# Reordering the first batch's opening, delaying one step of the second batch, and splitting the last output of a fused linear-attention and dense-experts kernel

## The chip, the core and the metric

The kernel runs on one core of one Trainium2 chip. The core has a matmul engine (TensorE, PE in the profile; its weight loads are listed as PEld), a vector engine (VectorE, DVE), an activation engine (ScalarE, ACT), a general engine (GpSimd, POOL), and SyncE (SP), which here only issues transfers. Each runs its own list of instructions in order and waits on semaphores for the others. Matmul results land in PSUM[...]. The metric is the device time of the whole program in microseconds (us); lower is better.

## What is computed

Eight batches of 512 tokens with 128 channels go through a linear attention block and then through eight dense experts, each with a layer norm before and after and a residual. All data are float32. This is the core of the reference:

```python
def attn(x, gamma, beta, w_qkv, w_out, b_out):        # x: (8, 512, 128)
    xn = (x - mean(x)) / sqrt(var(x) + 1e-5) * gamma + beta
    q, k, v = split(xn @ w_qkv, 3)                     # each as 4 heads of 32
    q = q * 32 ** -0.5
    k = softmax(k, axis=tokens)
    context = einsum('bnhd,bnhe->bhde', k, v)
    out = einsum('bhde,bnhd->bnhe', context, q)        # back to 128 channels
    return out @ w_out + b_out + x

def ffn(x, Wg, Wu, Wd):                                # 8 experts, hidden 512
    return sum(silu(x @ Wg[e]) * (x @ Wu[e]) @ Wd[e] for e in range(8))

x = x + layernorm(attn(layernorm(x), ...))
x = x + layernorm(ffn(layernorm(x), Wg, Wu, Wd))
```

## The kernel before

The work is staged by batch. The experts' part is a loop over *units*: a unit is one batch, but the first and the last batch are cut into two halves of 256 tokens each, so there are ten units. Every unit has 32 steps (8 experts by 4 slices of the hidden 512). A step multiplies the slice's `wg` and `wu` with the unit's normalised tokens `zT` (L572, L574), takes the silu of the first product on ACT (L576), multiplies the two on DVE (L578), and, two steps later, multiplies the result with `wd` into an accumulator bank (L532, function `down`). The tile framework is in manual schedule: every engine executes its instructions in exactly the order in which the program text issues them, and the framework only adds the waits.

Everything else is written as Python generators that are advanced once per step by `between`: `attention(b + 1)` for the next batch, `finish` for the output of the unit before, and for the first unit `prepare` (products of weights) and the rest of the first batch's second half. So a `yield` in one of these generators means "let one step of the experts go by".

`opening()` is the first batch's attention, which has no other work to hide behind. It works in two halves (`h` = 0, 1) of 256 tokens: statistics and normalisation on DVE (`xh`), transposes on PE (`xh_ps`), scale and shift on ACT (`xnT`); then for each half the product for `k` and the product for `v`; the maximum of `k` over the tokens (`kmax`, DVE) with copies of `v` on ACT; the products for `q`; the exponential of `k` (`ekT`, ACT); transposes of it (`ek_ps`) and copies (`ek`); the scaling of `q` (`qT`, ACT); and a one-element silu (`junk`) that makes ACT load the silu table. Then the chain `c_ps` (k times v), `ctxT` (mask to heads), `m_ps` (times w_out), `m` (divided by the softmax sum). `x1b` is the normalised input plus the output bias, added per 128 tokens on POOL (L303).

`after_wa` is the tail of attention for a range of tokens, again a generator: `y` = `q` times `m` on PE into the bank `y_ps` (L472) plus `x1b` on DVE (L476); statistics of `y`; `yn` and `x2`, the first residual; statistics of `x2`; `z`; transposes `z_ps`; and one ACT copy into `zT` (L495). `opening` advances the first half (`first`) to its end and the second half (`second`) up to its statistics; the rest of it runs during the first unit's steps. Five calls of `keep_warm` issue matmuls whose result is never read, two at the start and three in the tail.

In the attention of batch 1 (`b in BY_TENSORE`), the transposes of the exponential are copied from `ek_ps` to `ek` on DVE (L417), and one `yield` later the matmuls `g_ps` (L429) use it. In batches 2 to 7 the exponential goes through DRAM instead, and several steps are let by.

At the end of the program, the last unit's accumulator is copied whole to `fT` (L540, DVE), and `finish` transposes its two blocks of 128 tokens into one bank `f_ps`, takes statistics, normalises (`fn`), adds `x2` on POOL (L517) and issues one output transfer on SP's queue (L518).

Of the kernel before, what the change touches and what calls it, by code (L numbers as in the profile page):

```python
# [8 lines left out]
F32 = mybir.dt.float32  # L9
AF = mybir.ActivationFunctionType  # L10
# [5 lines left out]
def kernel(  # L16
# [223 lines left out]
    def flat(t):  # L240
        return t.rearrange("p j c -> p (j c)")
# [6 lines left out]
    def opening():  # L248


        b, xt = 0, xs[0]
        banks = [(ps, "ps"), (ps_gu, "g"), (ps_gu, "u")]
        turn = [0]

        def bank(name):
            pool, tag = banks[turn[0] % 3]
            turn[0] += 1
            return pool.tile([P, N], F32, tag=tag, name=f"{name}_{b}")
# [10 lines left out]
        x2s[0] = x2  # L269
        y = work.tile([P, NJ, C], F32, tag="y", name="y_0")  # L270
        yn = work.tile([P, NJ, C], F32, tag="yn", name="yn_0")
# [3 lines left out]
        ksum = small.tile([P, 3], F32, tag="ksum0", name="ksum_0")  # L275
        rsum = small.tile([P, 1], F32, tag="rsum", name="rsum_0")
        H = range(2)
        J = [slice(lo, hi) for lo, hi in HALVES]
        COL = [slice(lo * P, hi * P) for lo, hi in HALVES]
        W = N // 2  # L280

        keep_warm(warm, 2)
        keep_warm(w_qkv_sb[:, : N // 2])
# [5 lines left out]
        for h in H:  # L289
            norm_apply(xh[:, J[h]], xt[:, J[h]], (s1[h][0], s1[h][2]))  # L290
            t = bank(f"xh_ps{h}")
            for j in H:
                nc.tensor.transpose(t[:, j * P : (j + 1) * P], xh[:, 2 * h + j, :], ident)
            nc.scalar.activation(
                xnT[:, COL[h]], t[:, :W], AF.Identity, bias=beta_sb, scale=gamma_sb
            )
# [11 lines left out]
        for h in H:  # L308
            k_ps.append(bank(f"k_ps{h}"))
            nc.tensor.matmul(  # L310
                k_ps[h][:, :W], w_qkv_sb[:, C : 2 * C], xnT[:, COL[h]], start=True, stop=True
            )
            v_ps.append(bank(f"v_ps{h}"))
            for j in H:
                nc.tensor.matmul(
                    v_ps[h][:, j * C : (j + 1) * C],
                    xnT[:, (2 * h + j) * P : (2 * h + j + 1) * P], w_qkv_sb[:, 2 * C : 3 * C],
                    start=True, stop=True,
                )
        for h in H:  # L320
            nc.vector.tensor_reduce(kmax[:, h : h + 1], k_ps[h][:, :W], AX.X, ALU.max, negate=True)
            nc.scalar.copy(v[:, COL[h]], v_ps[h][:, :W])
        nc.vector.tensor_tensor(kmax[:, 2:3], kmax[:, 0:1], kmax[:, 1:2], ALU.min)
        for h in H:
            q_ps.append(bank(f"q_ps{h}"))
            nc.tensor.matmul(
                q_ps[h][:, :W], w_qkv_sb[:, 0:C], xnT[:, COL[h]], start=True, stop=True
            )
        for h in H:
            nc.scalar.activation(  # L330
                ekT[:, COL[h]], k_ps[h][:, :W], AF.Exp, bias=kmax[:, 2:3],
                accum_out=ksum[:, h : h + 1],
            )
        first_norm(1)
        for h in H:
            t = bank(f"ek_ps{h}")
            for j in H:
                nc.tensor.transpose(
                    t[:, j * P : (j + 1) * P], ekT[:, (2 * h + j) * P : (2 * h + j + 1) * P], ident
                )  # L340
            (nc.scalar.copy if h else nc.vector.tensor_copy)(ek[:, COL[h]], t[:, :W])
        for h in H:
            nc.scalar.mul(qT[:, COL[h]], q_ps[h][:, :W], QSCALE)
        nc.scalar.activation(junk, warm[:, :1], AF.Silu)
        nc.vector.tensor_tensor(ksum[:, 2:3], ksum[:, 0:1], ksum[:, 1:2], ALU.add)
        nc.vector.reciprocal(rsum, ksum[:, 2:3])
        c_ps = bank("c_ps")
        for j in range(NJ):
            nc.tensor.matmul(
                c_ps[:, :C], v[:, j * C : (j + 1) * C], ek[:, j * C : (j + 1) * C],  # L350
                start=(j == 0), stop=(j == NJ - 1),
            )
        ctxT = work.tile([P, C], F32, tag="ctxT", name="ctxT_0")
        nc.vector.tensor_tensor(ctxT, c_ps[:, :C], heads, ALU.mult)
        m_ps = bank("m_ps")
        nc.tensor.matmul(m_ps[:, :C], ctxT, w_out_sb, start=True, stop=True)
        m = work.tile([P, C], F32, tag="m", name="m_0")
# [18 lines left out]
    def attention(b):  # L376
# [38 lines left out]
        if b in BY_TENSORE:  # L415
            ek_ps = transpose4(ekT, f"ek_ps_{b}")
            nc.vector.tensor_copy(  # L417
                ek.rearrange("p b (j k) -> p j b k", j=NJ),
                ek_ps.rearrange("p (j b k) -> p j b k", j=NJ, b=NQ),
            )  # L420
# [47 lines left out]
    def after_wa(b, lo, hi, xt, xnT, wa, x1b, x2, y, yn, z, zT):  # L468
        r = slice(lo, hi)
        y_ps = ps.tile([P, N], F32, tag="ps", name=f"y_ps_{b}_{lo}")  # L470
        for j in range(lo, hi):
            nc.tensor.matmul(  # L472
                y_ps[:, (j - lo) * C : (j - lo + 1) * C], xnT[:, j * P : (j + 1) * P], wa,
                start=True, stop=True,
            )
        nc.vector.tensor_tensor(  # L476
            flat(y[:, r]), y_ps[:, : (hi - lo) * C], flat(x1b[:, r]), ALU.add
        )
# [13 lines left out]
        if b in BY_TENSORE:  # L492
            yield
            z_ps = transpose4(flat(z[:, r]), f"z_ps_{b}_{lo}")
            nc.scalar.copy(zT[:, :, r], by_block(z_ps[:, : (hi - lo) * P], hi - lo))  # L495
            zTs[b, lo] = zT[:, :, r]
# [5 lines left out]
    def finish(b, lo, hi, f):  # L502
# [15 lines left out]
        nc.sync.dma_start(out[b].rearrange("(p j) c -> p j c", j=NJ)[:, r], o[:, :n])  # L518

    units = [(b, lo, hi) for b in range(B) for lo, hi in parts(b)]  # L520
    NSTEP = E * NF
# [4 lines left out]
    def down(n, i):  # L526
# [19 lines left out]
    def between(n):  # L546
# [10 lines left out]
        for i in range(NSTEP):  # L557
            if i == LAG + 1 and n > 0:
                going.append(finish(*units[n - 1], fTs.pop(n - 1)))
            going = [g for g in going if next(g, "end") != "end"]  # L560
            yield

    opening()
# [57 lines left out]
```

## Time and profile before

| | us |
|---|---|
| median of 3 runs | 721.32 (721.27 to 721.45) |
| the profiled execution, its own time | 721.76 |
| its span, first to last instruction | 719.8 |
| PE busy in the span | 705.7 (98%) |
| DVE, ACT, POOL busy | 311.7, 200.9, 75.5 |

The profile is of one execution. Its span is divided by what it does: the opening ends with the first matmul of the experts (L572) at 22.70 us; from there the ten units follow one another until the last `down` matmul, at about 712.9; the end is what comes behind it. A row of the timeline gives the start in us, the duration, the engine, the line and the operation, and in brackets how long the engine had been idle before it and who released it. Float32 matmuls appear as two instructions each, so `x2` is one matmul. A busy engine is one with an instruction in flight; [...]the distance between the starts of two matmuls is shorter than the duration of one.

### The profile page before, as it was taken

What the parts mean: (1) busy time and instruction counts of PE and PEld (TensorE: products, weight loads), DVE (VectorE), ACT (ScalarE), POOL (GpSimd) and SP (SyncE); (2) the same over time, 40 slices, a digit from 0 to 9 for tenths busy, and PEclk for the clock granted to TensorE, in tenths of its full rate; (3) what the DMA queues carried; (4) which work ended last, traced back from release to release, by engine and by line L of the source; (5) the groups of instructions that cost most, each with busy time, mean ns of one, the idle gap of its engine ahead of it and who ended that gap; (6) DMA issues with size and microseconds to landing.
All of it is one profiled execution on the core that took longest, in us unless ns stands there. A gap on an engine that the chain in (4) does not pass through costs nothing. (4 is left out here: it accounts for less than half of the span.)

```text
span 719.8 us, 6734 instructions
## 1 busy us (share of the span) xinstructions
PE 705.7 (98%) x2177; PEld 397.7 (55%) x2177; DVE 311.7 (43%) x872; ACT 200.9 (28%) x378; POOL 75.5 (10%) x101
## 2 busy tenths in 40 slices
PE   7899999999999999999999999999999999999996
PEld 5788786444444544445444444444444454488885
DVE  4534545435345352444444444443534535243433
ACT  3323332422224122241223322242222412222221
POOL 3100111101002010020100110010100201000000
PEclk9999999999999999999999999999999999999999
DMA  8400000010110001110101101010001100000000
GB/s 268 145 1 0 23 1 15 22 31 0 44 60 34 11 15 29 59 45 0 45 8 51 45 0 44 30 45 30 0 29 47 42 15 12 18 31 15 8 1 8
DMA packets 27299, 23.83 MB, mean 33 GB/s; under 512 B 2944, under 2 KB 20480, under 8 KB 27264
## 3 DMA queue, kind: packets, MB, share of 16 engines
q1 hardware_dynamic: 27120, 23.28, 10.0%
q8 instruction: 17, 0.28, 0.2%
q14 instruction: 18, 0.15, 0.1%
q10 hardware_dynamic: 144, 0.13, 0.1%
HBM read 15.01 MB, written 8.39 MB: 33 GB/s over the span
## 5 line engine op out<-in xcount | busy, mean ns | idle before, releaser
L578 DVE TENSOR_TENSOR h<-sg,u 128x512 f32<-128x512 f32 (+1 forms) x320 | 185.4, 581 | 357.4 <-PE u L574 339.3
L576 ACT ACTIVATE sg<-g 128x512 f32<-128x512 f32 (+1 forms) x320 | 163.5, 511 | 481.8 <-PE g L572 445.1
L572 PE MATMUL g<-zT,wg 128*128 128x512 f32 (+1 forms) x640 | 272.6, 507 | 0.7 <-ACT zT L495 0.5
L574 PE MATMUL u<-zT,wu 128*128 128x512 f32 (+1 forms) x640 | 272.3, 507 | 0.0
L532 PE MATMUL acc<-h,wd 128*128 128x512 f32 (+1 forms) x640 | 272.1, 507 | 0.1
L532 PEld LDWEIGHTS acc<-h,wd 128*128 128x128 f32 x640 | 121.4, 190 | 99.3 <-issue 91.8
L574 PEld LDWEIGHTS u<-zT,wu 128*128 128x128 f32 x640 | 121.3, 190 | 98.9 <-issue 86.3
L572 PEld LDWEIGHTS g<-zT,wg 128*128 128x128 f32 x640 | 118.3, 190 | 84.5 <-issue 77.0
L172 POOL TENSOR_TENSOR rstd<-ve,mhalf 128x4 f32<-128x4 f32 (+1 forms) x28 | 25.9, 926 | 394.3 <-DVE ve L170 394.2
L194 POOL TENSOR_TENSOR rstd<-ve,mhalf 128x8 f32<-128x8 f32 x7 | 11.5, 1637 | 185.6 <-DVE ve L187 185.6
L412 POOL TENSOR_TENSOR x1b<-x,bias_sb 128x128 f32<-128x128 f32 x28 | 12.1, 462 | 23.1 <-DVE x L200 23.1
L517 POOL TENSOR_TENSOR o<-fn,x 128x512 f32<-128x512 f32 (+1 forms) x10 | 10.5, 1050 | 20.7 <-DVE fn L200 18.9
L200 DVE TENSOR_SCALAR x<-x,mv,rstd 128x128 f32<-128x128 f32 x32 | 11.1, 406 | 0.1
L483 POOL TENSOR_TENSOR x<-yn,x 128x512 f32<-128x512 f32 (+1 forms) x8 | 9.6, 1201 | 11.8 <-DVE yn L200 10.5
L200 DVE TENSOR_SCALAR xh<-x,mv,rstd 128x128 f32<-128x128 f32 x32 | 8.8, 336 | 2.1 <-POOL rstd L194 1.8
L429 PEld LDWEIGHTS g_ps<-ek,xh 128*128 128x128 f32 x56 | 7.3, 191 | 4.5 <-issue 2.9
L168 DVE BATCH_NORM_AGGREGATE mv<-stats 128x2 f32<-128x6 f32 x96 | 9.6, 157 | 0.0
L200 DVE TENSOR_SCALAR z<-x,mv,rstd 128x128 f32<-128x128 f32 x32 | 9.0, 341 | 1.3 <-POOL rstd L172 1.3
L200 DVE TENSOR_SCALAR yn<-y,mv,rstd 128x128 f32<-128x128 f32 x32 | 9.0, 341 | 1.3 <-POOL rstd L172 1.3
L476 DVE TENSOR_TENSOR y<-y_ps,x1b 128x512 f32<-128x512 f32 (+1 forms) x9 | 5.7, 632 | 8.2 <-PE y_ps L472 8.2
L404 ACT ACT_TABLE_LOAD x7 | 9.0, 1283 | 0.1
L576 ACT ACT_TABLE_LOAD x7 | 9.0, 1283 | 0.1
(115 smaller groups left out, 199.9 us busy)
## 6 DMA issues: line engine op xcount, KB each, us to landing
wg<-in_L_ffn_Wg_dram SPq DMA_DIRECT2D x8, 256.0 KB, 6.0
wu<-in_L_ffn_Wu_dram SPq DMA_DIRECT2D x8, 256.0 KB, 5.9
wd<-in_L_ffn_Wd_dram SPq DMA_DIRECT2D x8, 256.0 KB, 6.1
x<-in_L_attn_x_dram SPq DMA_DIRECT2D x7, 256.0 KB, 2.8
bounce<-xh_blk SPq DMA_DIRECT2D x6, 256.0 KB, 2.0
xhT<-bounce SPq DMA_DIRECT2D x24, 64.0 KB, 2.0
bounce<-ek_blk SPq DMA_DIRECT2D x6, 256.0 KB, 2.0
ek<-bounce SPq DMA_DIRECT2D x24, 64.0 KB, 2.0
```

Source lines behind the costliest of these rows:

```text
L168: nc.vector.bn_aggr(mv[:, j, :], stats[:, j, :])
L172: nc.gpsimd.tensor_tensor(rstd, ve, mhalf[:, :n], ALU.pow)
L194: nc.gpsimd.tensor_tensor(rstd, ve, mhalf, ALU.pow)
L200: nc.vector.tensor_scalar(dst[:, j], src[:, j], mv[:, j, 0:1], rstd[:, j : j + 1], ALU.subtract, ALU.mult,)
L412: nc.gpsimd.tensor_tensor(x1b[:, j, :], x1[:, j, :], bias_sb, ALU.add)
L483: (nc.gpsimd if b or lo else nc.vector).tensor_tensor(flat(x2[:, r]), flat(yn[:, r]), flat(xt[:, r]), ALU.add)
L517: nc.gpsimd.tensor_tensor(flat(o[:, :n]), flat(fn[:, :n]), flat(x2s[b][:, r]), ALU.add)
L532: nc.tensor.matmul(accs[n][:, :cols], wd_sb[e][:, f, :], hs.pop((n, i)), start=(i == 0), stop=(i == NSTEP - 1),)
L572: nc.tensor.matmul(g_ps[:, :cols], wg_sb[e][:, w], zT, start=True, stop=True)
L574: nc.tensor.matmul(u_ps[:, :cols], wu_sb[e][:, w], zT, start=True, stop=True)
L576: nc.scalar.activation(sg[:, :cols], g_ps[:, :cols], AF.Silu)
L578: nc.vector.tensor_tensor(h[:, :cols], sg[:, :cols], u_ps[:, :cols], ALU.mult)
```

## The change

The opening no longer takes its PSUM banks in turn from a list of three; every call of `bank` names its pool. The dummy matmuls at the start are four instead of two. Both products for `k` and their maxima are issued ahead of the products for `v`; the exponentials are issued ahead of the copies of `v`, and these copies move from ACT to DVE. The products for `q` and their scaling move behind `c_ps` and behind `m_ps`, one half each. For batch 0, `after_wa` adds `x1b` on PE: a matmul of the identity with `x1b` into `y_ps` comes first (for the first half ahead of the transposes of the exponential), the product `q` times `m` is accumulated on top, and statistics and normalisation read `y_ps` itself; the DVE addition is gone. One dummy matmul pair reads `xt` where it read `y`. The copy of the first half's transposed `z` is cut in two, one block on ACT, one on DVE. In the attention of batch 1 a second `yield` stands between `ek` and `g_ps`. The last unit gets a function of its own, `finish_last`, which copies, transposes, normalises, adds and stores its two blocks of 128 tokens one by one, the first block stored from SP's queue and the second from ACT's.

```diff
@@ -249,12 +249,9 @@
         b, xt = 0, xs[0]
-        banks = [(ps, "ps"), (ps_gu, "g"), (ps_gu, "u")]
-        turn = [0]
-
-        def bank(name):
-            pool, tag = banks[turn[0] % 3]
-            turn[0] += 1
+        def bank(name, tag):
+            pool = ps if tag == "ps" else ps_gu
             return pool.tile([P, N], F32, tag=tag, name=f"{name}_{b}")
 
...
-        y = work.tile([P, NJ, C], F32, tag="y", name="y_0")
+        y = {}
         yn = work.tile([P, NJ, C], F32, tag="yn", name="yn_0")
         z = work.tile([P, NJ, C], F32, tag="z", name="z_0")
         zT = work.tile([P, NQ, NJ, Q], F32, tag="zT", name="zT_0")
         kmax = small.tile([P, 3], F32, tag="kmax0", name="kmax_0")
         ksum = small.tile([P, 3], F32, tag="ksum0", name="ksum_0")
         rsum = small.tile([P, 1], F32, tag="rsum", name="rsum_0")
+        m = work.tile([P, C], F32, tag="m", name="m_0")
+        first, second = [
+            after_wa(b, lo, hi, xt, qT, m, x1b, x2, y, yn, z, zT) for lo, hi in HALVES
+        ]
         H = range(2)
         J = [slice(lo, hi) for lo, hi in HALVES]
         COL = [slice(lo * P, hi * P) for lo, hi in HALVES]
         W = N // 2
 
-        keep_warm(warm, 2)
+        keep_warm(warm, 4)
         keep_warm(w_qkv_sb[:, : N // 2])
         nc.scalar.copy(junk, warm[:, :1])
         s1 = [pair_stats(xt[:, J[h]], f"1_0_{h}") for h in H]
@@ -288,7 +289,7 @@
         q_ps = []
         for h in H:
             norm_apply(xh[:, J[h]], xt[:, J[h]], (s1[h][0], s1[h][2]))
-            t = bank(f"xh_ps{h}")
+            t = bank(f"xh_ps{h}", "g" if h else "ps")
             for j in H:
                 nc.tensor.transpose(t[:, j * P : (j + 1) * P], xh[:, 2 * h + j, :], ident)
             nc.scalar.activation(
@@ -306,63 +307,60 @@
 
         first_norm(0)
         for h in H:
-            k_ps.append(bank(f"k_ps{h}"))
+            k_ps.append(bank(f"k_ps{h}", "ps" if h else "u"))
             nc.tensor.matmul(
                 k_ps[h][:, :W], w_qkv_sb[:, C : 2 * C], xnT[:, COL[h]], start=True, stop=True
             )
-            v_ps.append(bank(f"v_ps{h}"))
+            nc.vector.tensor_reduce(kmax[:, h : h + 1], k_ps[h][:, :W], AX.X, ALU.max, negate=True)
+        nc.vector.tensor_tensor(kmax[:, 2:3], kmax[:, 0:1], kmax[:, 1:2], ALU.min)
+        for h in H:
+            nc.scalar.activation(
+                ekT[:, COL[h]], k_ps[h][:, :W], AF.Exp, bias=kmax[:, 2:3],
+                accum_out=ksum[:, h : h + 1],
+            )
+        for h in H:
+            v_ps.append(bank(f"v_ps{h}", "u" if h else "g"))
             for j in H:
                 nc.tensor.matmul(
                     v_ps[h][:, j * C : (j + 1) * C],
                     xnT[:, (2 * h + j) * P : (2 * h + j + 1) * P], w_qkv_sb[:, 2 * C : 3 * C],
                     start=True, stop=True,
                 )
+            nc.vector.tensor_copy(v[:, COL[h]], v_ps[h][:, :W])
+        next(first)
         for h in H:
-            nc.vector.tensor_reduce(kmax[:, h : h + 1], k_ps[h][:, :W], AX.X, ALU.max, negate=True)
-            nc.scalar.copy(v[:, COL[h]], v_ps[h][:, :W])
-        nc.vector.tensor_tensor(kmax[:, 2:3], kmax[:, 0:1], kmax[:, 1:2], ALU.min)
-        for h in H:
-            q_ps.append(bank(f"q_ps{h}"))
-            nc.tensor.matmul(
-                q_ps[h][:, :W], w_qkv_sb[:, 0:C], xnT[:, COL[h]], start=True, stop=True
-            )
-        for h in H:
-            nc.scalar.activation(
-                ekT[:, COL[h]], k_ps[h][:, :W], AF.Exp, bias=kmax[:, 2:3],
-                accum_out=ksum[:, h : h + 1],
-            )
-        first_norm(1)
-        for h in H:
-            t = bank(f"ek_ps{h}")
+            t = bank(f"ek_ps{h}", "u" if h else "g")
             for j in H:
                 nc.tensor.transpose(
                     t[:, j * P : (j + 1) * P], ekT[:, (2 * h + j) * P : (2 * h + j + 1) * P], ident
                 )
             (nc.scalar.copy if h else nc.vector.tensor_copy)(ek[:, COL[h]], t[:, :W])
-        for h in H:
-            nc.scalar.mul(qT[:, COL[h]], q_ps[h][:, :W], QSCALE)
-        nc.scalar.activation(junk, warm[:, :1], AF.Silu)
-        nc.vector.tensor_tensor(ksum[:, 2:3], ksum[:, 0:1], ksum[:, 1:2], ALU.add)
-        nc.vector.reciprocal(rsum, ksum[:, 2:3])
-        c_ps = bank("c_ps")
+        first_norm(1)
+        c_ps = bank("c_ps", "g")
         for j in range(NJ):
             nc.tensor.matmul(
                 c_ps[:, :C], v[:, j * C : (j + 1) * C], ek[:, j * C : (j + 1) * C],
                 start=(j == 0), stop=(j == NJ - 1),
             )
+        q_ps.append(bank("q_ps0", "u"))
+        nc.tensor.matmul(q_ps[0][:, :W], w_qkv_sb[:, 0:C], xnT[:, COL[0]], start=True, stop=True)
+        nc.scalar.mul(qT[:, COL[0]], q_ps[0][:, :W], QSCALE)
         ctxT = work.tile([P, C], F32, tag="ctxT", name="ctxT_0")
         nc.vector.tensor_tensor(ctxT, c_ps[:, :C], heads, ALU.mult)
-        m_ps = bank("m_ps")
+        m_ps = bank("m_ps", "ps")
         nc.tensor.matmul(m_ps[:, :C], ctxT, w_out_sb, start=True, stop=True)
-        m = work.tile([P, C], F32, tag="m", name="m_0")
+        q_ps.append(bank("q_ps1", "g"))
+        nc.tensor.matmul(q_ps[1][:, :W], w_qkv_sb[:, 0:C], xnT[:, COL[1]], start=True, stop=True)
+        nc.scalar.mul(qT[:, COL[1]], q_ps[1][:, :W], QSCALE)
+        nc.scalar.activation(junk, warm[:, :1], AF.Silu)
+        nc.vector.tensor_tensor(ksum[:, 2:3], ksum[:, 0:1], ksum[:, 1:2], ALU.add)
+        nc.vector.reciprocal(rsum, ksum[:, 2:3])
         nc.vector.tensor_scalar(m, m_ps[:, :C], rsum, None, ALU.mult)
-        first, second = [
-            after_wa(b, lo, hi, xt, qT, m, x1b, x2, y, yn, z, zT) for lo, hi in HALVES
-        ]
-        next(first)
         next(first)
         next(second)
-        keep_warm(flat(y[:, J[0]]), 2)
+        next(second)
+        keep_warm(flat(xt[:, J[0]]), 2)
+        next(first)
         next(first)
         keep_warm(flat(yn[:, J[0]]), 2)
         next(first)
@@ -418,6 +416,7 @@
                 ek.rearrange("p b (j k) -> p j b k", j=NJ),
                 ek_ps.rearrange("p (j b k) -> p j b k", j=NJ, b=NQ),
             )
+            yield
             yield
         else:
             to_tokens(by_block(ekT), ek, f"ek_blk_{b}")
@@ -468,18 +467,26 @@
     def after_wa(b, lo, hi, xt, xnT, wa, x1b, x2, y, yn, z, zT):
         r = slice(lo, hi)
         y_ps = ps.tile([P, N], F32, tag="ps", name=f"y_ps_{b}_{lo}")
+        if b == 0:
+            for j in range(lo, hi):
+                cols = slice((j - lo) * C, (j - lo + 1) * C)
+                nc.tensor.matmul(y_ps[:, cols], ident, x1b[:, j, :], start=(j == lo), stop=False)
+            yield
         for j in range(lo, hi):
             nc.tensor.matmul(
                 y_ps[:, (j - lo) * C : (j - lo + 1) * C], xnT[:, j * P : (j + 1) * P], wa,
-                start=True, stop=True,
-            )
-        nc.vector.tensor_tensor(
-            flat(y[:, r]), y_ps[:, : (hi - lo) * C], flat(x1b[:, r]), ALU.add
-        )
-        yield
-        s3 = norm_stats(y[:, r], f"3_{b}_{lo}")
-        yield
-        norm_apply(yn[:, r], y[:, r], s3)
+                start=(b > 0), stop=(b > 0 or j == hi - 1),
+            )
+        if b == 0:
+            y[lo] = y_ps[:, : (hi - lo) * C].rearrange("p (j c) -> p j c", c=C)
+            yb = y[lo]
+        else:
+            yb = y[:, r]
+            nc.vector.tensor_tensor(flat(yb), y_ps[:, : (hi - lo) * C], flat(x1b[:, r]), ALU.add)
+        yield
+        s3 = norm_stats(yb, f"3_{b}_{lo}")
+        yield
+        norm_apply(yn[:, r], yb, s3)
         (nc.gpsimd if b or lo else nc.vector).tensor_tensor(
             flat(x2[:, r]), flat(yn[:, r]), flat(xt[:, r]), ALU.add
         )
@@ -492,7 +499,12 @@
         if b in BY_TENSORE:
             yield
             z_ps = transpose4(flat(z[:, r]), f"z_ps_{b}_{lo}")
-            nc.scalar.copy(zT[:, :, r], by_block(z_ps[:, : (hi - lo) * P], hi - lo))
+            for j in range(hi - lo if b == 0 and lo == 0 else 1):
+                cp = nc.vector.tensor_copy if j else nc.scalar.copy
+                if b or lo:
+                    cp(zT[:, :, r], by_block(z_ps[:, : (hi - lo) * P], hi - lo))
+                else:
+                    cp(zT[:, :, j], z_ps[:, j * P : (j + 1) * P].rearrange("c (a i) -> c a i", a=NQ))
             zTs[b, lo] = zT[:, :, r]
         else:
             to_channels(z, zT.rearrange("c a j i -> c a (j i)"), f"z_blk_{b}")
@@ -517,6 +529,44 @@
         nc.gpsimd.tensor_tensor(flat(o[:, :n]), flat(fn[:, :n]), flat(x2s[b][:, r]), ALU.add)
         nc.sync.dma_start(out[b].rearrange("(p j) c -> p j c", j=NJ)[:, r], o[:, :n])
 
+    def finish_last(b, lo, hi, acc):
...
+        acc = acc.rearrange("c (a j i) -> c a j i", a=NQ, j=n)
+        dst = out[b].rearrange("(p j) c -> p j c", j=NJ)
+        f_ps = []
+        for j in range(n):
+            cols = slice(j * P, (j + 1) * P)
+            (nc.scalar.copy if j else nc.vector.tensor_copy)(
+                fT[:, cols].rearrange("c (a i) -> c a i", a=NQ), acc[:, :, j]
+            )
+            t = ps.tile([P, N], F32, tag="ps", name=f"f_ps_last{j}")
+            nc.tensor.transpose(t[:, :P], fT[:, cols], ident)
+            f_ps.append(t)
+        for j in range(n):
+            nc.vector.bn_stats(stats[:, j, :], f_ps[j][:, :C])
+        for j in range(n):
+            nc.vector.bn_aggr(mv[:, j, :], stats[:, j, :])
+        nc.vector.tensor_scalar_add(ve, mv[:, :, 1], EPS)
+        nc.gpsimd.tensor_tensor(rstd, ve, mhalf[:, :n], ALU.pow)
+        for j in range(n):
+            nc.vector.tensor_scalar(
+                fn[:, j, :], f_ps[j][:, :C], mv[:, j, 0:1], rstd[:, j : j + 1],
+                ALU.subtract, ALU.mult,
+            )
+            (nc.vector if j else nc.gpsimd).tensor_tensor(
+                o[:, j, :], fn[:, j, :], x2s[b][:, lo + j], ALU.add
+            )
+            (nc.scalar if j else nc.sync).dma_start(dst[:, lo + j], o[:, j, :])
     units = [(b, lo, hi) for b in range(B) for lo, hi in parts(b)]
     NSTEP = E * NF
     LAG = 2
@@ -534,7 +584,11 @@
             start=(i == 0), stop=(i == NSTEP - 1),
         )
         if i == NSTEP - 1:
-            acc = accs.pop(n)[:, :cols].rearrange("c (a j i) -> c a j i", a=NQ, j=hi - lo)
+            acc = accs.pop(n)[:, :cols]
+            if n == len(units) - 1:
+                finish_last(b, lo, hi, acc)
+                return
+            acc = acc.rearrange("c (a j i) -> c a j i", a=NQ, j=hi - lo)
             if hi - lo < NJ:
                 fT = work.tile([P, N], F32, tag="fT", name=f"fT_{n}")
                 nc.vector.tensor_copy(by_block(fT[:, :cols], hi - lo), acc)
@@ -585,8 +640,6 @@
             pass
     while pending:
         down(*pending.pop(0))
-    for _ in finish(*units[-1], fTs.pop(len(units) - 1)):
-        pass
 
 
 # ---- launch: one core; inputs and outputs as the reference has them ----
```

More of the change, by code (lines that the diff above doesn't have):

```diff
@@ L518, in finish @@
         nc.sync.dma_start(out[b].rearrange("(p j) c -> p j c", j=NJ)[:, r], o[:, :n])
+    def finish_last(b, lo, hi, acc):
+        n = hi - lo
+        stats = small.tile([P, n, 6], F32, tag=f"stats{n}", name="stats_last")
+        mv = small.tile([P, n, 2], F32, tag=f"mv{n}", name="mv_last")
+        rstd = small.tile([P, n], F32, tag=f"rstd{n}", name="rstd_last")
+        ve = small.tile([P, n], F32, tag=f"ve{n}", name="ve_last")
+        fT = work.tile([P, N], F32, tag="fT", name="fT_last")
+        fn = work.tile([P, NJ, C], F32, tag="fn", name="fn_last")
+        o = work.tile([P, NJ, C], F32, tag="o", name="o_last")
+        acc = acc.rearrange("c (a j i) -> c a j i", a=NQ, j=n)
[24 more added lines that the diff above has]
+            (nc.scalar if j else nc.sync).dma_start(dst[:, lo + j], o[:, j, :])
     units = [(b, lo, hi) for b in range(B) for lo, hi in parts(b)]
@@ L561, in between @@
             yield
+        assert not going
     opening()
```

## The prediction, made before the changed kernel had run

> **What bounds the kernel now.** I read the page's totals first (PE busy 98% of the span), then busy time by stage, since 98% is an average over stages with different limits.
>
> ```profile
> core 0: us, PE busy (x) PEld busy (x) DVE busy (x) ACT busy (x) POOL busy (x), PEclk, DMA share, GB/s
> 0.00:22.70 22.70, 16.72 (x63) 11.21 (x63) 11.70 (x51) 7.06 (x16) 7.98 (x23) 1.00 0.90 285
> 60.00:106.00 46.00, 44.40 (x215) 37.25 (x214) 24.95 (x89) 15.83 (x36) 8.09 (x10) 1.00 0.04 9
> 106.00:712.90 606.90, 606.90 (x1727) 316.62 (x1725) 259.41 (x687) 165.70 (x293) 56.57 (x64) 1.00 0.08 26
> 712.90:719.80 6.90, 0.45 (x3) 0.20 (x2) 2.04 (x8) 0.00 (x0) 1.43 (x2) 0.83 0.05 19
> ```
>
> From 106 to 712.9 us PE never stops; the change neither adds nor removes matmuls there, so nothing can come from that stretch. What is left is the opening (22.7 us), the end (6.9 us), and 1.6 us of idle PE between 60 and 106. The waits of PE name the last:
>
> ```profile
> PE g_ps L429 <- DVE ek L417: 1.2, 1, 1.2
> ```
>
> In the opening and the end each engine waits for the one before it. The timeline, on which every later term rests, in pieces:
>
> ```profile
> 9.08 1.06 PE L310 MATMUL k_ps<-xnT,w_qkv_sb 128*128 128x256 f32 x2
> 10.18 0.43 DVE L321 TENSOR_REDUCE kmax<-k_ps 128x1 f32<-128x256 f32 x1 [1.28 <-PE k_ps L310]
> 11.03 0.37 ACT L322 COPY v<-v_ps 128x256 f32<-128x256 f32 x1 [1.33 <-PE v_ps L315]
> 11.30 0.48 ACT L330 ACTIVATE ekT<-k_ps,kmax 128x256 f32<-128x256 f32 x1
> ...
> 16.25 0.42 DVE L476 TENSOR_TENSOR y<-y_ps,x1b 128x256 f32<-128x256 f32 x1 [0.94 <-PE y_ps L472]
> 16.70 0.49 DVE L166 BATCH_NORM_STATS2 stats<-y 128x6 f32<-128x128 f32 x2
> ...
> 22.27 0.37 ACT L495 COPY zT<-z_ps 128x256 f32<-128x256 f32 x1 [6.97 <-PE z_ps L209]
> 22.70 0.70 PE L572 MATMUL g<-zT,wg 128*128 128x256 f32 x2 [0.46 <-ACT zT L495]
> ```
>
> The chain is k's second product, its maximum, the exponential (held until 11.30 though the maximum is ready at 10.80: ACT is in the copy of v), transposes, c, m, y, two norms, zT. Two groups by form show PE's clock:
>
> ```profile
> L310 PE MATMUL k_ps<-xnT,w_qkv_sb 128*128 128x256 f32 x4 | 2.2, 654 | 0.0
> L326 PE MATMUL q_ps<-xnT,w_qkv_sb 128*128 128x256 f32 x4 | 1.1, 397 | 0.0
> ```
>
> The same shape takes 654 ns for k and 397 for q. Passes of k and v start 0.43 us apart, those of q (from 10.79) 0.21: PE runs at half rate until about 10.8. (The PEclk column does not show it.)
>
> **The opening, up to the exponential.** The second half's `xnT` is ready at 8.10 in either version. Before, PE is then in the first v product, and k starts at 9.08. After, k starts at 8.23: -0.85. ACT's copy of v is no longer ahead of the exponential: -0.45. The four dummy matmuls instead of two keep PE busy from 1.18 to about 6.0 without a gap (8 passes of 0.43, then the w_qkv pair of 1.19, which starts at about 5.0 behind them instead of 4.21). That may delay the first transposes from 5.83 to 6.0; the second pair (6.77) and hence `xnT` at 8.10 stay. If it also brings the full rate forward to about 7.5, k takes 0.60 instead of 1.06: -0.46. Then the exponential starts at 9.54, 1.76 earlier, and v, `ek` and c follow in step (v on PE 8.66 to 9.7; its copies on DVE, two of 0.43 by `kmax`'s and `y`'s rows, end at about 10.4, ahead of the first `ek` copy at 10.6).
>
> Does it come forward? The row: 2.1 us of dummies, a gap of 1 us and 1.2 us more left PE at half rate; the uninterrupted stretch from 6.8 to 10.8 raised it. [...] I take it as the likeliest case (A), not as sure. In case B the rate rises at 10.8 as before: PE is in v until 10.79, then adds `x1b` (two 128-column products, 0.43), the transposes start at 11.25 instead of 11.92, and the gain up to here is 0.67 instead of 1.76.
>
> **The moves that cost nothing, and their cover.** The first q product (0.43) lies in the 0.63 between c's last pass and `m_ps` (drain, `ctxT` 0.29, waits), the second in the 0.65 between `m_ps` and y (`m` 0.35): covered; without the cover 0.4 each. `qT` has 0.35 on ACT, and y of the first half needs only the first. The silu table load (1.28 plus 0.20) moves behind the second `qT`, to about 13.9 to 15.3; ACT's next work is zT at about 20. The trace puts y's start (15.45) down to this silu, but `m` also ends at 15.30, and y reads `m`, not `junk`. The second normalisation for `x1` (0.60 on DVE) moves behind the `ek` copy, its POOL additions (0.90) end near 12.7; the PE addition that reads them is queued at about 14.1. The first one waits for POOL at 8.49 and stands ahead of the transposes of `ekT`: free in A. SP's weight loads are not moved; the first units' weights have landed by then, as the absence of DMA among PE's waits says.
>
> **The tail of the opening.** The DVE addition goes: 16.25 to 16.70 = -0.45. Normalising `yn` out of PSUM: the row for `fn<-f_ps` has 404 ns against 341 for `yn<-y`, a pair in 0.73 against 0.60: +0.13; the statistics cost the same (0.50 against 0.49). The split zT copy: by the widths, two engines with 0.27 and 0.29 instead of 0.37, -0.08. [...] No trace here shows two readers; but it does show that statistics on the first block of `f_ps` (713.90) wait for the transposes of both blocks of that bank (713.86). [...] I take +0.25; the range holds -0.08.
>
> Opening in A: -1.76 - 0.45 + 0.13 + 0.25 = -1.83. In B: -0.67 - 0.32 + 0.25 = -0.74.
>
> **The first units.** `y_ps` of the second half is now held until its `yn` is done on DVE in the first step, about 2.3 us behind the first g. If the next products of `prepare` (wq, bv) need that bank, PE waits from 1.1 to 2.4: +1.3 with all of the experts queued behind. Banks are given out in the order in which they came free, which makes it mb's bank; mb waits for `bvw` until 2.3 anyway. I take 0, with 1.3 as the other end.
>
> **Batch 1's extra step.** `g_ps` can start at 79.20, when `ek` is copied. After, g, u and down of one more step go first: g at 77.84, u held by the bank of an `h` that ends at 78.54 (0.35), down until 79.48, `g_ps` until 80.34. Before, the same work ends at 81.38. That is -1.04 of the 1.19. What is late next: DVE, with the `h` at 79.07, in time for its reader at 80.3. The later steps of batch 1 move by 1.3 us in a unit with steps to spare.
>
> **The end.** Before:
>
> ```profile
> 712.94 0.42 DVE L540 COPY fT<-acc 128x256 f32<-128x256 f32 x1 [0.80 <-PE acc L532]
> 713.90 0.50 DVE L166 BATCH_NORM_STATS2 stats<-f_ps 128x6 f32<-128x128 f32 x2 [0.53 <-PE f_ps L209]
> ...
> 715.64 0.73 DVE L200 TENSOR_SCALAR fn<-f_ps,mv,rstd 128x128 f32<-128x128 f32 x2 [0.82 <-POOL rstd L172]
> 716.50 0.72 POOL L517 TENSOR_TENSOR o<-fn,x 128x256 f32<-128x256 f32 x1 [0.90 <-POOL rstd L172]
> 717.25 0.33 SPq L518 DMA_DIRECT2D out_dram<-o  x1
> ```
>
> After, even with one-bank copies in sequence, the second block is copied at 713.54, transposed at 713.88, in the statistics by 714.17 instead of 714.40: -0.23. From `fn` to the store it was 1.61 us; now `fn` 0.73 for both, the second addition on DVE 0.29, 0.08 of waits: 1.10, while the first block goes through POOL (0.46) beside it: -0.51. Two transfers of 64 KB instead of one of 128 KB, the later one issued from ACT: the opening's halves of x landed in 2.6 from SP and 2.8 from ACT, and an ACT issue took 0.41 against 0.37; I add 0.1 (0 to 0.5). End: -0.65.
>
> **The sum.** A: -1.83 - 1.04 - 0.65 = -3.5. B: -2.4. The profiled execution took 721.76 for a span of 719.77; A makes that 718.2. It lies 0.44 above the median of the runs, 721.32, to which the forecast is put: 717.8.
>
> **The rivals.**
> B, the rate does not come forward: [...] against it, the gap is gone. 721.32 - 2.4 = 718.9.
> C, a bank is the new wait (B's opening and PE held by `y_ps` for 1.3): 720.0; if in A, 719.1. For: `y_ps` lives three steps longer. Against: the order of freeing.
> D, slower: the tail now reads PSUM and its dummies are fewer in the gaps, so PE stands idle and drops to half rate as the experts begin. [...] A's gain and 1.44 on top are 4.9[...]. For: half rate exists here. Against: the longest idle stretch of PE I foresee in the tail is about 1.5 us (before: 1.33 ahead of `yn`, and the rate stayed full).
> E, the order on the engines comes out as before because the waits tie the moved pieces together: only end and batch 1 remain, 721.32 - 1.7 = 719.6.
>
> **How the numbers follow.** A 0.58, B 0.22, C 0.08, E 0.06, D 0.06. A's own range is 716.9 (copies in parallel, and the xh transposes also at full rate, 0.3 each) to 718.6. With B it reaches 719.0; a part of E and of C in A takes it to 719.6. Below 0.2% (1.44 us) this kernel can't be told from no change: faster means below 719.88. That is A, B, E and half of C, less some of E over the line: 0.88; same 0.06, slower 0.06.
>
> **What would show it.** First g at about 20.9 (B: 22.0); passes of the k products 0.21 apart (B: 0.43); exponential at 9.5; no L476 for batch 0; zT's DVE piece starting behind ACT's; no wait of PE for `ek`, 0.4 or less for `h`; last store issued 0.7 closer behind the last `acc`. A first g at 22.5 or later, or a wait of PE on DVE above 1 us in the first two steps, would make the forecast wrong.

## The result

The changed kernel takes 718.15 us (median of 6 runs, 718.01 to 718.32) against 721.44 for the one before in the same comparison: a ratio of 0.9952, 95% interval 0.994 to 0.9965, 3.3 us less. The forecast was 717.8, with a range that reaches from 716.9 to 719.6.

The profiled execution took 718.09 us, its span 715.99, which is 3.79 shorter than before. Busy time by stage, cut at the first matmul of the experts (20.47) and at the end of the last `down` matmul (709.70), with a stretch of 46 us around batch 1's attention between:

```profile
core 0: us, PE busy (x) PEld busy (x) DVE busy (x) ACT busy (x) POOL busy (x), PEclk, DMA share, GB/s
0.00:20.47 20.47, 16.88 (x75) 11.49 (x75) 12.06 (x52) 6.51 (x14) 7.96 (x23) 1.00 0.87 277
57.80:103.80 46.00, 45.44 (x220) 38.06 (x219) 25.36 (x90) 15.88 (x37) 8.09 (x10) 1.00 0.03 9
103.80:709.70 605.90, 605.90 (x1722) 316.00 (x1720) 258.82 (x686) 165.61 (x292) 56.44 (x64) 1.00 0.08 26
709.70:716.00 6.30, 0.62 (x2) 0.28 (x2) 2.33 (x9) 0.27 (x1) 1.16 (x2) 0.72 0.07 21
```

The opening is 2.23 us shorter (22.70 to 20.47). The experts take 689.23 from first matmul to last (709.70 - 20.47) against 690.21, 0.98 shorter. The end takes 6.28 against 6.86, 0.58 shorter. 2.23 + 0.98 + 0.58 = 3.79: the whole span. Over the long stretch PE is as full as it was.

PE's waits from the first expert matmul to the last show what became of the wait for `ek`:

```profile
PE g L627 <- DVE zT L507: 0.7, 1, 0.7
PE g L627 <- ACT sg L631: 0.3, 1, 0.3
PE u L629 <- DVE h L633: 0.2, 1, 0.2
```

The 1.2 us for `ek` is gone and 0.2 for `h`, in batch 1's extra step, is new. The wait for `zT` was 0.5 behind ACT and is 0.7 behind DVE. The timeline of the opening, at the places that were shown of before:

```profile
7.05 1.52 PE L311 MATMUL k_ps<-xnT,w_qkv_sb 128*128 128x256 f32 x4
8.61 0.42 DVE L314 TENSOR_REDUCE kmax<-k_ps 128x1 f32<-128x256 f32 x1 [0.41 <-PE k_ps L311]
9.26 0.47 ACT L317 ACTIVATE ekT<-k_ps,kmax 128x256 f32<-128x256 f32 x1 [1.44 <-DVE kmax L315]
...
13.40 0.68 PE L476 MATMUL y_ps<-m,qT 128*128 128x128 f32 x4
...
14.12 0.50 DVE L166 BATCH_NORM_STATS2 stats<-y_ps 128x6 f32<-128x128 f32 x2 [0.87 <-PE y_ps L476]
...
19.83 0.27 ACT L507 COPY zT<-z_ps 128x128 f32<-128x128 f32 x1 [4.59 <-PE z_ps L209]
20.12 0.29 DVE L507 COPY zT<-z_ps 128x128 f32<-128x128 f32 x1 [0.72 <-ACT zT L507]
20.47 0.70 PE L627 MATMUL g<-zT,wg 128*128 128x256 f32 x2 [0.68 <-DVE zT L507]
```

The exponential is 2.04 us earlier, y 2.05, and ACT's and DVE's pieces of `zT` stand one behind the other. By form, the k products are no longer at the half rate (654 ns before):

```profile
L311 PE MATMUL k_ps<-xnT,w_qkv_sb 128*128 128x256 f32 x4 | 1.4, 428 | 0.1
```

The end, in the same view:

```profile
709.73 0.29 DVE L548 COPY fT_last<-acc 128x128 f32<-128x128 f32 x1 [0.80 <-PE acc L582]
710.06 0.27 ACT L548 COPY fT_last<-acc 128x128 f32<-128x128 f32 x1 [1.67 <-DVE fT_last L548]
...
712.28 0.73 DVE L561 TENSOR_SCALAR fn_last<-f_ps_last,mv_last,rstd_last 128x128 f32<-128x128 f32 x2 [0.82 <-POOL rstd_last L559]
712.77 0.45 POOL L565 TENSOR_TENSOR o_last<-fn_last,x 128x128 f32<-128x128 f32 x1 [0.53 <-DVE fn_last L561]
713.05 0.33 DVE L565 TENSOR_TENSOR o_last<-fn_last,x 128x128 f32<-128x128 f32 x1
713.25 0.33 SPq L568 DMA_DIRECT2D out_dram<-o_last  x1
713.41 0.35 ACTq L568 DMA_DIRECT2D out_dram<-o_last  x1
```

Here too the two copies out of one bank follow one another (709.73 + 0.29, then 710.06). The last store is issued 3.71 us behind the last `acc` instead of 4.34.

### The profile page after: what moved, and what is told of

It reads as the page before. It is cut to its first block, busy times and chain, and to the rows that moved or that the text cites. A ratio compares the mean times of both kernels' runs of the same rounds, so it can differ in the third digit from the quotient of the medians.

```text
span 716.0 us, 6760 instructions
## 1 busy us (share of the span) xinstructions
PE 706.1 (99%) x2189; PEld 398.4 (56%) x2189; DVE 312.3 (44%) x874; ACT 200.6 (28%) x377; POOL 75.1 (10%) x101
## 5 line engine op out<-in xcount | busy, mean ns | idle before, releaser
L490 POOL TENSOR_TENSOR x<-yn,x 128x512 f32<-128x512 f32 (+1 forms) x8 | 9.6, 1199 | 12.2 <-DVE yn L200 10.8
L476 PEld LDWEIGHTS y_ps<-wa,xnT 128*128 128x128 f32 x56 | 7.4, 192 | 2.9 <-issue 2.9
```

The lines of the kernel that those rows point to most:

```text
L490: (nc.gpsimd if b or lo else nc.vector).tensor_tensor(flat(x2[:, r]), flat(yn[:, r]), flat(xt[:, r]), ALU.add)
```

## The experiments

All were timed in five rounds. Those of one group shared the runs of the kernel before; the changed kernel itself (718.15) was timed apart from them. The kernel before had medians of 721.8, 721.47 and 721.56 in the three groups, and the 95% intervals of the ratios to it overlap that of the changed kernel in every experiment but one (the kernel before with four dummies). So what a part is worth is read from the stage of the profile that it touches; the difference of medians stands beside it, and one of 0.3 us or less says nothing.

### 1. The parts taken back one by one

**Two dummy matmuls instead of four.**

```diff
-        keep_warm(warm, 4)
+        keep_warm(warm, 2)
```

> The changed kernel with two dummy matmuls at the start instead of four, all else kept. In the changed kernel's profile the passes of k are already at the full rate (starts 0.21 us apart). Theory: the two extra dummies close the gap at the start and bring the full rate forward, and the order alone does not. Then the k and v products run at half rate again (k's mean about 650 ns against 380), the exponential starts at about 10.0 instead of 9.3, the transposes at 11.0 to 11.3 instead of 9.9, and the kernel takes 1.0 to 1.3 us longer than the changed one: about 719.3. Rival: k's order is what counts, and the rate is worth little: within 0.3 us of the changed kernel, 718.2 to 718.5.

719.12 us (718.89 to 720.0), 0.97 above the changed kernel; ratio to before 0.9966 (0.9953 to 0.9978). In its profile k is at half rate, and the exponential starts at 10.05, y at 14.20, and the first g at 21.27, 0.80 later than in the changed kernel:

```profile
7.28 2.08 PE L311 MATMUL k_ps<-xnT,w_qkv_sb 128*128 128x256 f32 x4
9.15 1.20 PE L324 MATMUL v_ps<-w_qkv_sb,xnT 128*128 128x128 f32 x8
10.05 0.47 ACT L317 ACTIVATE ekT<-k_ps,kmax 128x256 f32<-128x256 f32 x1 [1.97 <-DVE kmax L315]
10.19 0.61 PE L473 MATMUL y_ps<-x1b,ident 128*128 128x128 f32 x4
10.67 0.90 PE L334 MATMUL ek_ps<-ident,ekT 128*128 128x128 f32 x4
```

The k pair takes 2.08; v, the same amount of work, takes 1.20: the full rate came in the middle, at 9.4. This is the prediction's case B in kind (it had the rate rise at 10.8).

**One yield in batch 1.**

```diff
                 ek_ps.rearrange("p (j b k) -> p j b k", j=NJ, b=NQ),
             )
-            yield
             yield
```

> The changed kernel with one yield between ek and g_ps in batch 1, as before. Theory: PE's wait for ek at g_ps (1.2 us) comes back and nothing else changes: +1.0 us against the changed kernel, 719.2. Rival: the opening now starts 2.2 us earlier and shifts the work beside it, so that the wait would not have been there anyway: within 0.2 us of the changed kernel.

719.09 us (718.88 to 719.22), 0.94 more; ratio to before 0.9963 (0.995 to 0.9977). In its profile the experts take 690.18 from first matmul to last, against 689.23, and PE's waits have the old line back:

```profile
PE g_ps L427 <- DVE ek L415: 1.2, 1, 1.2
```

**The end as before.** In `down`, the branch to `finish_last` is taken out and the closing loop over `finish` put back.

> The changed kernel with the last unit finished as before: one copy of the accumulator, one bank, one addition on POOL, one store. Theory: from the last down matmul to the end of the span 6.9 us instead of 6.3, so +0.6 us, 718.8. Rival: the end is set by the fixed landing time of a store, and two stores give back what the earlier issue gains: within 0.2 us.

718.54 us (718.23 to 718.64), 0.4 more by the medians; ratio to before 0.9955 (0.9943 to 0.9968). In the profile the last store is issued 4.33 us behind the last `acc` and the span ends 2.53 behind the store, 6.86 in all, as in the kernel before; in the changed kernel it is 3.71 and 2.58, 0.57 less. Two stores of 64 KB landed in 1.6 each, one of 128 KB in 1.7: the landing hardly changed, and the gain is in the earlier issue.

### 2. zT: one bank, one copy or two

**One copy.** The loop over blocks is replaced:

```diff
-            for j in range(hi - lo if b == 0 and lo == 0 else 1):
...
+            nc.scalar.copy(zT[:, :, r], by_block(z_ps[:, : (hi - lo) * P], hi - lo))
```

> The changed kernel with the first half's zT copied by ACT in one piece, as before. In the changed profile DVE's piece starts when ACT's is done (20.12 behind 19.83 + 0.27). Theory: the two pieces run one behind the other because they read one bank, so that one copy of 0.37 is shorter: first g 0.2 us earlier behind the z transposes (0.80 instead of 1.04 behind the end of z_ps being written is not needed; the gap from z_ps start to g goes from 1.26 to 1.05), 717.9 to 718.0. Rival: the first piece lets something start earlier, so the split pays: 718.2 to 718.4.

717.99 us (717.73 to 718.12), which the medians can't tell from 718.15; ratio to before 0.9948 (0.9936 to 0.9961). The profile can: from the first z transpose to the first g 1.05 us (19.38 to 20.43), against 1.26 in the changed kernel (19.21 to 20.47). This part of the change costs 0.21.

**Two banks.**

```diff
-            z_ps = transpose4(flat(z[:, r]), f"z_ps_{b}_{lo}")
+            if b or lo:
+                z_ps = [transpose4(flat(z[:, r]), f"z_ps_{b}_{lo}")]
+            else:
+                z_ps = [transpose4(z[:, j], f"z_ps_{b}_{j}") for j in range(lo, hi)]
```

The copies then read one of the two each, ACT the first and DVE the second.

> The changed kernel with the first half's two z transposes in two banks, each copied by its engine. Theory: the bank alone forced the copies one behind the other; with a bank each ACT copies while PE transposes the second block and DVE copies it right behind, so from the first z transpose to the first g about 0.95 us, against 1.26 in the changed kernel and 1.05 with one copy: 717.8. Rival: what separates the copies is not the bank: 1.26 stays.

718.09 us (717.65 to 719.26); ratio to before 0.9954 (0.9942 to 0.9967). The first copy now starts while PE works on the second transpose, and the second waits for PE instead of ACT:

```profile
19.26 0.58 PE L209 MATMUL z_ps<-ident,z 128*128 128x128 f32 x2 [0.18 <-DVE z L200]
19.62 0.27 ACT L509 COPY zT<-z_ps 128x128 f32<-128x128 f32 x1 [4.34 <-PE z_ps L209]
19.88 0.29 DVE L509 COPY zT<-z_ps 128x128 f32<-128x128 f32 x1 [0.42 <-PE z_ps L209]
20.27 0.67 PE L631 MATMUL g<-zT,wg 128*128 128x256 f32 x2 [0.43 <-ACT zT L509]
```

From z to g 1.01 us, where I had expected 0.95. The first copy starts 0.36 behind the first transpose instead of 0.62, and DVE no longer waits for ACT. So it was the shared bank that held the first copy until both transposes were done and the second copy until the first was done. The copies still don't overlap (19.62 + 0.27, then 19.88), because DVE's block is transposed only then: the gain is the earlier first copy. With a bank each the split is 0.25 shorter than with one bank, but only 0.04 shorter than one copy.

### 3. x1b on DVE

In `after_wa` the identity matmuls are taken out, `y` is a tile again, and the DVE addition is back for batch 0; the first half's statistics are issued ahead of the second half's addition.

```diff
-            for j in range(lo, hi):
-                cols = slice((j - lo) * C, (j - lo + 1) * C)
-                nc.tensor.matmul(y_ps[:, cols], ident, x1b[:, j, :], start=(j == lo), stop=False)
...
+        yb = y[:, r]
+        nc.vector.tensor_tensor(flat(yb), y_ps[:, : (hi - lo) * C], flat(x1b[:, r]), ALU.add)
```

> The changed kernel with x1b added on DVE for batch 0, statistics and normalisation reading y in SBUF, and no identity matmuls; the statistics of the first half are issued ahead of the second half's addition. Theory: +0.45 for the addition and -0.13 for normalising out of SBUF, so +0.3, about 718.5; from the first y matmul to the first g 7.4 us instead of 7.07. Rival: reading PSUM or the two more matmuls on PE cost as much as the addition: no difference.

718.55 us (718.3 to 720.61); ratio to before 0.9964 (0.9951 to 0.9976). From the first y matmul to the first g 7.46 us (13.50 to 20.96) against 7.07 (13.40 to 20.47): 0.39 for the addition on PE, within 0.1 of the prediction's 0.32.

### 4. The order and the rate

The prediction had added the order (0.85 for k ahead of v, 0.45 for the exponential ahead of the copies) and the rate (0.46). Four kernels test that sum.

**The kernel before with four dummies**, one line of the change (`keep_warm(warm, 4)`) alone.

> The kernel before with four dummy matmuls at the start instead of two, and nothing else of the change. The prediction counted 0.85 for k ahead of v, 0.45 for the exponential ahead of the copies and 0.46 for the rate as a sum. Theory: they are not a sum. With the full rate from 4 to 7 us on, a v product takes 0.43 and fits between k's first product and the moment when xnT's second half is ready, so the rate alone brings most of the 2.0: y starts at 13.4 to 13.7 and the kernel gains 1.7 to 2.0 us on the one before. Rival (the sum of the prediction): only 0.5 us.

720.02 us (719.76 to 721.66, 21 runs), 1.45 less than before; ratio 0.9981 (0.9974 to 0.9987). The size was between the theory's 1.7 to 2.0 and the rival's 0.5. Twenty of the runs lie between 719.76 and 720.12; the 21st, at 721.66, is the profiled one, and it shows why: there the full rate came only at 10.8, dummies or not, and the opening is that of the kernel before (exponential at 11.31, first g at 22.70). No execution of this kernel with the early rate was profiled, so where in the opening its 1.45 lies is not shown.

```profile
L310 PE MATMUL k_ps<-xnT,w_qkv_sb 128*128 128x256 f32 x4 | 2.2, 662 | 0.0
```

**The changed kernel with the old order** of k, v and the exponential (q stays late):

```diff
+        for h in H:
+            nc.vector.tensor_reduce(kmax[:, h : h + 1], k_ps[h][:, :W], AX.X, ALU.max, negate=True)
+            nc.scalar.copy(v[:, COL[h]], v_ps[h][:, :W])
...
-            nc.vector.tensor_copy(v[:, COL[h]], v_ps[h][:, :W])
```

(with the v products moved back into the loop over k).

> The changed kernel (four dummies, q late) with the k and v products alternating and the copies of v on ACT ahead of the exponential, as before. Theory: at the full rate the order is worth little: y starts 0 to 0.2 us later than in the changed kernel, 718.1 to 718.4. Rival (the sum of the prediction): the order is worth 1.3 us at any rate, 719.4.

718.08 us (717.9 to 719.71), by the medians the same as the changed kernel; ratio to before 0.9957 (0.9944 to 0.9971). In the profile y starts at 13.79, the exponential at 9.64 behind a copy of v that ends at 9.75 by its own row; y is 0.2 to 0.3 later than in kernels of the new order whose rate rose as late (13.50 and 13.58). A v product, short now, goes between the two k products:

```profile
7.32 0.70 PE L311 MATMUL k_ps<-xnT,w_qkv_sb 128*128 128x256 f32 x2
7.85 0.61 PE L316 MATMUL v_ps<-w_qkv_sb,xnT 128*128 128x128 f32 x4
8.30 0.60 PE L311 MATMUL k_ps<-xnT,w_qkv_sb 128*128 128x256 f32 x2
9.64 0.48 ACT L326 ACTIVATE ekT<-k_ps,kmax 128x256 f32<-128x256 f32 x1
```

k's second product starts at 8.30, where the prediction had 8.23 for the new order. The v product still holds it up a little: the second half's `xnT` is done at 7.87, and k's second maximum starts at 8.93, against 8.70 in the kernel of experiment 3, whose `xnT` is done at 7.91.

**The old order with two dummies.**

> The changed kernel with two dummies and with k and v alternating and v copied on ACT first: the fourth corner of a square with the changed kernel (new order, four: 718.15), two dummies (new order, two: 719.12) and the old order (old, four: 718.08). Theory: at the half rate a v product takes 0.85 and does not fit ahead of k's second product, so here the order counts: y starts at about 15.4 as before instead of 14.20, 1.0 to 1.3 us more than with two dummies alone, 720.1 to 720.4. Rival: the order is worth nothing at either rate: 719.1.

719.65 us (718.88 to 720.13, 6 runs); ratio to before 0.997 (0.9958 to 0.9983). The profiled execution is the slowest of them (rate at 12.6, exponential at 11.42, y at 15.81). The square of medians:

| us | two dummies | four dummies |
|---|---|---|
| old order | 719.65 | 718.08 |
| new order | 719.12 | 718.15 |

By these medians the dummies are worth 1.6 in the old order and 1.0 in the new. The order is worth nothing at four dummies and 0.5 at two, where I had expected 1.0 to 1.3; but the runs at two overlap (718.88 to 720.13 and 718.89 to 720.0), so that 0.5 is not shown. The medians may mix executions whose rate rose at different times; a profile shows a single execution and when its rate rose. The time from the first statistics of x to the exponential in the four profiles, with the rise of the rate in brackets:

| us | two dummies | four dummies |
|---|---|---|
| old order | 3.52 to 11.42: 7.90 (12.6) | 3.31 to 9.64: 6.33 (6.6) |
| new order | 3.38 to 10.05: 6.67 (9.4) | 3.27 to 9.26: 5.99 (6.0) |

With two dummies k ran at the half rate to its end in both, and there the order brings 1.23, close to the 1.30 that were booked for it (the kernel before has 7.90 as well: 3.40 to 11.30). With four it brings 0.34, or 0.30 against the kernel of experiment 3, whose rate rose later too (7.1; 3.33 to 9.36). The rate brings 1.57 in the old order and 0.68 in the new. So the two edits do largely the same work: whichever comes first takes most of it.

**q ahead of the transposes.**

```diff
+        for h in H:
+            q_ps.append(bank(f"q_ps{h}", "g" if h else "ps"))
+            nc.tensor.matmul(
+                q_ps[h][:, :W], w_qkv_sb[:, 0:C], xnT[:, COL[h]], start=True, stop=True
+            )
         next(first)
```

(and out of the two later places).

> The changed kernel with both q products ahead of the x1b addition and the transposes of the exponential, right behind v; the scalings of q stay where they are. The prediction gave this move no worth. Theory: that holds only for the half rate, where the exponential ended after q (11.78 against 11.65); at the full rate the two q products (0.86 with the addition behind them) end at about 10.6, when the exponential is there at 9.9, so the transposes and the rest of the chain come 0.6 to 0.8 us later: 718.8. Rival (the prediction's word): nothing, 718.1 to 718.2.

718.96 us (718.85 to 719.03), 0.8 more; ratio to before 0.9961 (0.9949 to 0.9974). The exponential is where it was (9.32), but PE is busy:

```profile
9.36 1.03 PE L332 MATMUL q_ps<-xnT,w_qkv_sb 128*128 128x256 f32 x4
10.22 0.61 PE L474 MATMUL y_ps<-x1b,ident 128*128 128x128 f32 x4
10.67 0.60 PE L339 MATMUL ek_ps<-ident,ekT 128*128 128x128 f32 x4
```

The transposes start at 10.67 instead of 9.88, y at 14.13 instead of 13.40, and the first g at 21.21 instead of 20.47.

### 5. A version that takes what the runs pointed to

Two banks for z, and five dummies without the pair on w_qkv:

```diff
-        keep_warm(warm, 4)
-        keep_warm(w_qkv_sb[:, : N // 2])
+        keep_warm(warm, 5)
```

> Two banks for the z transposes, and five dummies on the constant tile without the pair on w_qkv. Theory: without that pair's wait for the group before it, PE is free at 5.5 to 5.7 instead of 5.8 to 6.2, when the first block to transpose is ready at 5.7, and the full rate comes as often: 717.7 to 717.9. Rival: the activity that counts gets shorter (4.4 us instead of 4.9), the full rate comes late in more runs, and the median is no better than 718.1.

717.91 us (717.74 to 718.13); ratio to before 0.9947 (0.9935 to 0.996). It has the lowest median of all, clearly below the kernel before; against the changed kernel (0.9952) the intervals overlap, so a gain on it is not shown. The dummies end at 5.2 and the first transposes start at 5.78 when their input is ready, where they started at 6.01 in the changed kernel. That is not owed to the missing pair: with the pair, and the rate up as early (5.2), the first kernel with two banks starts them at 5.74, and its y starts at 13.45 against 13.49 here.

## Why the prediction was right, step by step

**The total and its parts.** Predicted -3.5 for the span, measured -3.79: opening -1.83 against -2.23, batch 1 -1.04 against -0.98, end -0.65 against -0.58. The executed medians moved by 3.3: the profiled execution of the kernel before (721.76) lay 0.3 above its median here, and the time outside the span was 1.99 in it and 2.10 in the changed one's.

**The clock, case A.** Held: k's mean fell from 654 to 428 ns. (The two passes of a product started 0.3 apart, where 0.43 stood before and 0.21 had been given as the sign.) That A was the likeliest case was my estimate, not shown by the trace of before. The doubt held as well: with four dummies the rate can still come late, at 10.8 in the one profile at 721.66. Case B was put at 1.1 above A; two dummies measured 0.97, with a rise at 9.4 instead of 10.8.

**The sum in front of the exponential.** Its total of 1.76 was close to the 2.04 measured (0.13 of the difference is x landing earlier in this execution, statistics at 3.27 instead of 3.40; the rest is the transposes of `xh` at the full rate, which the prediction kept only for its range). From `xnT` to the exponential the prediction had 1.44 (8.10 to 9.54), and 1.44 was measured (7.82 to 9.26). Its terms hold in the order in which it counted them, the order of the products first, at the half rate (1.30 booked, 1.23 measured), and the rate on top (0.46 booked, 0.68 measured, the transposes included). As the worth of each edit they are wrong. "Before, PE is then in the first v product, and k starts at 9.08. After, k starts at 8.23: -0.85" is true only while a v product takes 0.85. At the full rate it takes 0.44 and delays k's second maximum by about 0.2. So, once the rate is up, the order is worth 0 (by the medians) to 0.3 (by the profile), and the rate alone is worth 1.4 to 1.6. The sum came out because the terms were counted one after the other along one path.

**"The moves that cost nothing".** The later q products are covered, as said: `ctxT` starts at 12.03 as c ends, and `m_ps` at 12.38. But the prediction gave the move no worth, and it has 0.7 (by the profile) to 0.8: in the kernel before, q ended (11.65) ahead of the exponential (11.78) and stood in no one's way; with an exponential 2 us earlier it would have been the next thing late.

**The tail.** Addition on PE: 0.32 predicted, 0.39 measured. Split zT: +0.25 predicted, as 0.27 + 0.05 + 0.29 against 0.37, with the copies one behind the other; that they would run so was my estimate, not shown by the trace of before. +0.21 was measured, and two banks took it away; the widths alone had promised -0.08. The trace shows DVE's copy released by ACT's (19.83 + 0.27, then 20.12); in none of the profiles do the two copies run at once in one bank, so what would happen then is not shown.

**The first units.** No wait of PE on DVE in the first two steps: `mb_ps` started 2.38 behind the first g (2.42 before), waiting for ACT's `bvw`. Rival C did not come, nor E. D did not come: PE's longest wait in the tail was 0.9 us, for `yn`, where 1.3 stood before, and the record of the granted rate has no fall between its rise at 5.97 and 712.53, behind PE's last matmul.

**Batch 1.** The one step more gained 0.94 to 0.98 for 1.04 predicted, with the foreseen wait for `h` at 0.2 instead of 0.35.

**The end.** The store is issued 0.63 earlier behind the last `acc` (0.74 worked out), less 0.06 for landing (0.1). The statistics gave 0.15 of it, where 0.23 had been worked out; from `fn` to the issue it takes 1.13 instead of 1.61, as worked out (1.10).

**Slips that did not count.** The prediction says that passes of k and v start 0.43 apart at the half rate. That holds for k; v's are half as wide and start 0.21 apart (a product of two took 0.85, as it says). C's 720.0 should be 720.2 (718.9 + 1.3), and A's lower end, from the two terms named, 717.2 instead of 716.9.

## What to carry to other kernels

Before adding up the gains of several edits on one path, ask of each whether it would still gain if the others were already in: reordering pays for a stage that is late, and a faster stage can make the order nearly idle (and can make a move worthwhile that was idle before, as q's). Splitting a copy over two engines cost 0.21 us here out of one bank, and with a bank for each half it gained only 0.04. Where PE stands behind a `yield` for another engine's copy, one more step of independent work in between removed nearly the whole wait here (1.2 us, with 0.2 for `h` in its place).

## What the runs showed of the hardware that I had not expected

How reliably the dummies bring the full rate. Each trace records when the granted rate rose and when it fell again, to 0.5, behind the last work: in the kernel before at 10.92 and at 717.48, where PE's last matmul ends at 713.86, in the changed one at 5.97 and at 712.53, where it ends at 710.70. The PEclk column counts what lies before the first record as full (1.00 for 0 to 20.47), and so doesn't show the rise. With four or five dummies it came at 4.1, 4.5, 4.9, 4.9, 5.2, 6.0, 6.6, 6.9 and 7.1 us in nine executions and at 10.8 in one; with two dummies (the kernel before included) at 9.4, 10.9 and 12.6. What decides when it comes is not shown: in the execution with 7.1 (the end as before) and in the one with 10.8 PE had done the same up to 6.03, dummies from 1.18 to 4.96, the pair on w_qkv from 5.0 to 6.2. Single runs 1.2 to 2 us above the others of their kernel (719.71, 719.26, 720.61) would fit a late rate, but those were not the profiled ones, so for them it is not shown.
